# Gated cross-attention on one core: two squares placed five products later, and two steps of the last quad moved

## The chip, the cores and the metric

The kernel runs on one core of a Trainium2 chip. A core has a matrix engine (TensorE, in the profile PE, its weight loads PEld), a vector engine (VectorE, DVE), a scalar engine (ScalarE, ACT), a general engine (GpSimd, POOL) and a queue engine (SyncE, SP) that here only issues DMA transfers. Each engine works through its own list of instructions in order; semaphores make one wait for another. Matmul results go to PSUM, which is divided into banks; everything else lies in SBUF. The metric is the time of one execution on the device in microseconds (us); less is better.

## What is computed

Eight batches of 1024 tokens of width 1024 (x), and for each batch 64 memory rows of width 512:

```python
memory_proj = einsum('bme,de->bmd', memory, W_mem)
scores = einsum('bnd,bmd->bnm', hidden_states, memory_proj) / sqrt(D)
attn = softmax(scores, axis=-1)
memory_context = einsum('bnm,bmd->bnd', attn, memory_proj)
gate_input = concatenate([hidden_states, memory_context], axis=-1)
gate = sigmoid(einsum('bnf,df->bnd', gate_input, W_gate) + b_gate)
fused = hidden_states + gate * memory_context
out = fused * rsqrt(mean(fused ** 2, axis=-1) + 1e-6) * norm_w
```

All of it is in 32-bit floating point. Nearly all the arithmetic is the half of the gate's matmul that multiplies x with the first 1024 columns of W_gate.

## The kernel before

**Quads and products.** The 8192 tokens are worked on in 16 quads (`NQ`) of 512 tokens. In a quad, x times the gate's weights is done by a Strassen-like scheme: seven outer products, in the order `ORDER = (1, 6, 7, 5, 4, 2, 3)`, and inside each outer product seven inner products of 256 columns. An inner product is one slot of the schedule, so a quad has 49 slots (`SLOTS`), and outer products 1, 6, 7, 5, 4, 2 and 3 start at slots 0, 7, 14, 21, 28, 35 and 42 of the quad. A quad's four output tiles of 128 tokens are `O[q, 0]` to `O[q, 3]`, called gate in the profile; tiles 0 and 1 are row 0, tiles 2 and 3 row 1.

**One outer product** (`outer_product`, L880). Its first inner product fills a quarter of PSUM bank `af`, and ScalarE copies that to `u` (L901). The second goes to bank `kB`, the third to `kC`; VectorE adds each onto u in turn. Four more inner products accumulate in `ed` and again in `af`. The sixth and seventh reach the same `af` tile that the L901 copy reads, and so stand behind that copy. Steps on the output tiles follow: `pre` on GpSimd, `fin_ed` and `fin_af` on VectorE.

**The visits.** Row 1 is finished in product 4, row 0 in product 3 (`SECOND`). There, after the third inner product, TensorE makes a visit (`visit`, L820): a run of small matmuls with the attention, into banks `pc` and onto `af` and `ed`. They take the banks b and c that kB and kC used, so the VectorE adds onto u have to have read these. During the visit TensorE runs no inner product; this is the visit's gap. After it the sigmoid on ScalarE (L685), the product with pc on VectorE (`gated`), and what follows for the row.

**After a row is finished**, for all quads but the last: five slots later GpSimd issues a DMA that adds x from memory onto each tile (`residual`, L687). Later, ScalarE squares each of the two tiles with a sum along the row (`square`, L699) and takes the square root of both sums (L704, with its table load). VectorE takes the reciprocal (L710) and multiplies each half of a tile with it and with norm_w (`norm`, L714: halves (c, 0), (c, 1), (d, 0), (d, 1) of tiles c and d of the row); after the second half of a tile SyncE stores it to out. Row 0's steps fall in the next quad.

**The order of the work** is written by hand. `at(slot, ...)` puts a step on a list for a slot, and `step()` issues the list just ahead of that slot's matmuls; `mid(key, ...)` puts one at a fixed place inside an outer product: `(q, 4, 0)` is after the visit's matmuls have been issued and before `fin_af`, `(q, 3)` lies after the visit. The tuple `when` in `outer_product` holds the slots of the two squares and the four norms, counted from the end of product 3 or 4; `None` and -2 are places in the middle of the next quad's products 4 and 3, and -1 is `(q + 1, 4, 0)`. In a quad, the ones that matter here on ScalarE are the u copy of product 7 (slot 14), row 0's squares of the quad before (17, 18), the four attnT copies of the transposed attention (`transpose_attn`, slot 18, L472), and the u copies of products 5 and 4 (slots 21 and 28).

**The last quad** adds x by VectorE from a tile `xl`, which one DMA of 2 MB loads (`load_last`, L730; it takes the buffer of the quads' `xq`). Its norms follow slots of their own.

Of the kernel before, what the change touches and what calls it, by code (L numbers as in the profile page):

```python
# [20 lines left out]
def tile_gated_cross_attention_rmsnorm(  # L21
# [47 lines left out]
    NQ = B * QPB  # L69
# [546 lines left out]
    def at(slot, fn, *args):  # L616
        due.setdefault(slot, []).append(lambda: fn(*args))

    def mid(key, fn, *args):
        beside.setdefault(key, []).append(lambda: fn(*args))  # L620
# [5 lines left out]
    def plan(q):  # L626
        t0 = SLOTS * q
        nxt = q + 1 < NQ
        for i, o in enumerate(ORDER):
            for part, t in ((0, 1), (1, 2)):  # L630
                if i + 1 < len(ORDER):
                    at(t0 + 7 * i + t, inner_s, q, ORDER[i + 1], part)
                elif nxt:
                    at(t0 + 7 * i + t, inner_s, q + 1, ORDER[0], part)
        if q == 0:
            at(t0 + 7, scores, q)
            at(t0 + 8, add_scores, q)
        at(t0 + (3 if q else 7), outer_s, q, 3)
        at(t0 + (11 if q else 22), outer_s, q, 4)
        at(t0 + 9, transpose_scores, q)  # L640
        at(t0 + 10, softmax_a, q)
        at(t0 + 13, softmax_b, q)
        at(t0 + 18, transpose_attn, q)
        at(t0 + 22, attn_difference, q)
        if not nxt:
            at(t0 + 5, load_last)
            return
        at(t0 + 2, load_xq, q + 1)
        for i, t, half in (
            (20, 0, 0), (21, 1, 0), (23, 2, 0), (25, 3, 0), (37, 2, 1), (38, 3, 1), (42, 0, 1)  # L650
        ):
            at(t0 + i, transpose_x, q + 1, t, half)
        mid((q, 3, 1), transpose_x, q + 1, 1, 1)
        mid((q, 3), scores, q + 1)
        at(t0 + 46, add_scores, q + 1)
        mid((q, 3), outer_s, q + 1, 1)
        mid((q, 3), outer_s, q + 1, 2)
        if (q + 1) % QPB == 0:
            at(t0 + 10, load_mp, (q + 1) // QPB)
            at(t0 + 49, load_mg, (q + 1) // QPB)  # L660
        if q == 0:
            at(t0 + 8, add_bias, mgs[0][M:P, :])
            at(t0 + 20, add_bias, mgd[1, M:, :])
# [128 lines left out]
    def sqrt_table():  # L792

        t = t4k(small, [P, 1], "warm", "warm")
        pin(nc.scalar.activation(t, eps_sb, AF.Sqrt))
# [84 lines left out]
    def outer_product(q, o):  # L880
# [78 lines left out]
        if second and not nxt:  # L959
            c, d = 2 * row, 2 * row + 1  # L960
            if o == 3:
                sqrt_table()
            when = (3, 4, 4, None, 10, 11) if o == 4 else (0, 2, 2, 2, 3, 3)
            if o == 4:
                for h_ in range(2):
                    mid((q, 3, 0), last_weigh, c, h_)
            at(slot + when[0], last_root, d)
            at(slot + when[1], last_root, c)
            for w_, (t, h_) in zip(when[2:], ((d, 0), (d, 1), (c, 0), (c, 1))):
                if w_ is None:  # L970
                    mid((q, 3, 0), last_norm, t, h_)
                else:
                    at(slot + w_, last_norm, t, h_)
        elif second:

            c, d = 2 * row, 2 * row + 1
            for t in (d, c):
                at(slot + 5, residual, q, t)
            if row == 0:
                when = (17, 18, -1, None, 33, -2) if q + 2 < NQ else (17, 18, 20, 22, 24, 25)  # L980
            else:
                when = (17, 18, 22, 24, 29, 31)
            at(slot + when[0], square, q, c)
            at(slot + when[1], square, q, d)
            for w_, (t, h_) in zip(when[2:], ((c, 0), (c, 1), (d, 0), (d, 1))):
                if w_ is None:
                    mid((q + 1, 4), norm, q, t, h_)
                elif w_ < 0:
                    mid((q + 1, 4, 0) if w_ == -1 else (q + 1, 3), norm, q, t, h_)
                else:  # L990
                    at(slot + w_, norm, q, t, h_)
        del L2[q, o]

    for q in range(NQ):
        plan(q)
        for o in ORDER:
            outer_product(q, o)
# [29 lines left out]
```

## Time and profile before

| | |
|---|---|
| median of three executions | 956.16 us (955.21 to 956.31) |
| the profiled execution | 956.04 us |
| its span, first to last instruction | 954.0 us |
| TensorE's granted clock | 0.996 of full speed |
| ScalarE: squares, L699 | 60 of 1057 ns, idle before them 16.9 us |
| ScalarE: u copies, L901 | 112 of 364 ns |
| VectorE: norms, L714 | 120 of 987 ns |
| residual DMA, 512 KB | 60, median 8.4 us from issue to landing |
| xl DMA, 2 MB | one, 10.1 us from issue to landing |

The profile is of one execution; its span is 2.04 us shorter than the time of that execution. A group of instructions is named by the line of the kernel and by the tiles that it writes and reads, so that `gate<-in_x` is a residual, `junk<-gate` a square and `u<-af` a copy of the first inner product. A wait is put down to what came last by the profile. The ends of matmuls are modelled, so a busy TensorE isn't one at its peak; the distance between the starts of the same step in two quads is the better measure.

### The profile page before, as it was taken

How to read it: one execution, taken by the hardware profiler on the slowest of the kernel's cores; microseconds unless marked ns; L12 is line 12 of the kernel's file. 1: busy time of each engine (PE TensorE's matmuls, PEld its weight loads, DVE VectorE, ACT ScalarE, POOL GpSimd, SP SyncE). 2: the span in 40 equal slices, each digit the busy share in tenths (PEclk: the TensorE clock that was granted, in tenths of full speed). 3: DMA queues.
4: the chain of work that ended last, by engine and by line, in shares of the span. 5: the costliest groups of instructions: out<-in, count | busy, mean ns of one | idle time of the engine just before them, and what ended most of it. 6: DMA issues, size and time to landing. Idle time of an engine off the chain costs nothing.

```text
span 954.0 us, 15598 instructions
## 1 busy us (share of the span) xinstructions
PE 940.2 (99%) x5624; PEld 730.9 (77%) x5624; DVE 807.5 (85%) x1258; ACT 362.9 (38%) x782; POOL 710.3 (74%) x780
## 2 busy tenths in 40 slices
PE   9999999999999999999999999999999999999995
PEld 8546778787877778787877778687877778787773
DVE  6988888888888888888888888888888888888887
ACT  3001235262533425162433526252443526253456
POOL 4998877678676767788676767777686767877683
PEclk9999999999999999999999999999999999999998
DMA  9856674482919365481919365391918466390812
GB/s 377 276 151 156 110 127 107 114 174 54 200 45 193 96 135 120 109 179 44 212 45 178 89 144 133 91 196 30 217 53 164 103 131 146 77 211 25 220 66 89
DMA packets 70924, 128.41 MB, mean 135 GB/s; under 512 B 12352, under 2 KB 49216, under 8 KB 70592
## 3 DMA queue, kind: packets, MB, share of 16 engines
q1 hardware_dynamic: 61664, 93.86, 37.2%
q0 software_dynamic: 9184, 33.56, 19.2%
q8 instruction: 45, 0.74, 0.3%
q14 instruction: 31, 0.25, 0.1%
HBM read 87.56 MB, written 41.68 MB: 135 GB/s over the span
## 4 chain that ended last, share of the span: by engine, by line
PE 91%; DMA 4%; ACT 1%; DVE 1%; POOL 1%; issue 1%; SPq 0%; DVEq 0%
PE af L92 29%; PE ed L92 19%; PE pc L92 10%; PE kC L92 9%; PE kB L92 9%; PE pg L92 5%; PE psT_af L92 5%; DMA gate<-in_x 3%; PE pm L92 2%; POOL l L95 1%; DMA wm<-in_w_mem_t 1%; PE psT_ed L92 0%; ACT attnT L472 0%; PE psT_b L92 0%; DVE gate L714 0%
## 5 line engine op out<-in xcount | busy, mean ns | idle before, releaser
L95 POOL TENSOR_TENSOR gate<-gate,u 128x512 f32<-128x512 f32 (+1 forms) x224 | 237.0, 1071 | 189.7 <-DVE u L95 153.8
L685 ACT ACTIVATE gate<-gate 128x512 f32<-128x512 f32 x128 | 80.2, 630 | 224.3 <-DVE gate L95 224.3
L352 DVE STREAM_TRANSPOSE a<-xq 128x512 f32<-128x512 f32 x128 | 141.5, 1108 | 3.0 <-POOL it L95 3.0
L95 POOL TENSOR_TENSOR l<-a 128x256 f32<-128x256 f32 x128 | 112.9, 882 | 18.7 <-PE af L92 17.4
L714 DVE SCALAR_TENSOR_TENSOR gate<-gate,ss,nw_sb 128x512 f32<-128x512 f32 x120 | 118.4, 987 | 1.1
L92 PE MATMUL pc<-mg,attnT 64*64 64x512 f32 x512 | 116.8, 595 | 0.3 <-DVE u L95 0.3
L92 PE MATMUL ed<-it,l 128*128 128x256 f32 x448 | 115.0, 379 | 0.0
L92 PE MATMUL kB<-it,l 128*128 128x256 f32 x448 | 115.0, 379 | 0.0
L95 DVE TENSOR_TENSOR gate<-gate,pc 128x512 f32<-128x512 f32 x128 | 86.2, 682 | 31.7 <-ACT gate L685 31.7
L901 ACT COPY u<-af 128x256 f32<-128x256 f32 x112 | 40.8, 364 | 187.0 <-PE af L92 185.9
L92 PE MATMUL af<-w,a 128*128 128x256 f32 x384 | 98.5, 379 | 0.0
L92 PEld LDWEIGHTS kB<-it,l 128*128 128x128 f32 x448 | 85.1, 190 | 11.6
L95 DVE TENSOR_TENSOR gate<-gate,ed 128x512 f32<-128x512 f32 x112 | 76.1, 679 | 19.5 <-POOL gate L95 17.8
L92 PEld LDWEIGHTS ed<-it,l 128*128 128x128 f32 x448 | 83.9, 190 | 10.7
L95 DVE TENSOR_TENSOR gate<-gate,af 128x512 f32<-128x512 f32 (+1 forms) x128 | 76.9, 611 | 13.4 <-PE af L92 11.9
L92 PEld LDWEIGHTS af<-w,a 128*128 128x128 f32 x384 | 73.0, 190 | 10.3 <-issue 0.5
L95 POOL TENSOR_TENSOR l<-s 128x256 f32<-128x256 f32 x96 | 78.4, 816 | 3.1 <-PE af L92 3.1
L92 PEld LDWEIGHTS pc<-mg,attnT 64*64 64x64 f32 x512 | 32.9, 132 | 50.2 <-issue 23.5
L699 ACT ACTIVATE junk<-gate 128x1024 f32<-128x1024 f32 x60 | 63.5, 1058 | 16.9 <-DMA gate<-in_x 15.9
L92 PE MATMUL af<-mg,attnT 64*64 64x256 f32 (+1 forms) x384 | 67.4, 456 | 0.0
L92 PE MATMUL ed<-it,a 128*128 128x256 f32 x256 | 67.4, 386 | 0.0
L95 DVE TENSOR_TENSOR u<-u,kC 128x256 f32<-128x256 f32 x112 | 46.0, 410 | 23.7 <-PE kC L92 20.3
(147 smaller groups left out, 2043.4 us busy)
## 6 DMA issues: line engine op xcount, KB each, us to landing
xq<-in_x SPq DMA_DIRECT2D x64, 512.0 KB, 10.3
gate<-in_x POOLq DMA_DIRECT2D x60, 512.0 KB, 8.4
out<-gate SPq DMA_DIRECT2D x60, 512.0 KB, 3.0
w<-in_w_gate_t SPq DMA_DIRECT2D x8, 512.0 KB, 10.2
w<-in_w_gate_t SPq DMA_DIRECT2D x2, 2048.0 KB, 16.5
mg<-mgd SPq DMA_DIRECT2D x16, 256.0 KB, 5.5
wm<-in_w_mem_t SPq DMA_DIRECT2D x4, 512.0 KB, 6.0
mpd<-mpT SPq DMA_DIRECT2D x4, 512.0 KB, 7.7
```

The source lines that it names most:

```text
L92: pin(nc.tensor.matmul(o, lhsT, rhs, start=start, stop=stop, skip_group_check=True))
L95: pin(eng.tensor_tensor(o, a, b, op))
L352: nc.vector.transpose(A[key][:, :, r * P : (r + 1) * P], chunks(xq[q][:, 4 * t : 4 * t + 4, :], KD)[:, half * KH : (half + 1) * KH],)
L685: pin(nc.scalar.activation(g, g, AF.Sigmoid))
L699: nc.scalar.activation(junk, O[q, t], AF.Square, accum_out=ss[:, t % 2 : t % 2 + 1])
L714: nc.vector.scalar_tensor_tensor(g[:, cols], g[:, cols], rstd[:, t % 2 : t % 2 + 1], nw_sb[:, cols], ALU.mult, ALU.mult,)
L901: pin(nc.scalar.copy(p1, af[:, 0]))
```

## The change

```diff
@@ plan @@
         if not nxt:
-            at(t0 + 5, load_last)
+            at(t0 + 12, load_last)
             return
@@ outer_product @@
             if row == 0:
-                when = (17, 18, -1, None, 33, -2) if q + 2 < NQ else (17, 18, 20, 22, 24, 25)
+                when = (22, 23, -1, None, 33, -2) if q + 2 < NQ else (17, 18, 20, 22, 24, -1)
             else:
                 when = (17, 18, 22, 24, 29, 31)
```

Three things are moved, and none is added or taken away.

The squares of row 0 go from slots 17 and 18 of the next quad to slots 22 and 23. This holds for the rows of quads 0 to 13, which are squared in quads 1 to 14. On ScalarE the two squares, the load of the sqrt table and the sqrt stood between the u copy of product 7 and the attnT copies; now they stand behind the u copy of product 5 and ahead of that of product 4. The norms that use them keep their places.

In the last quad, `load_last` goes from slot 5 to slot 12. On SyncE the load of xl now stands behind the store of tile 2 of quad 14, and ahead of that of tile 3.

For row 0 of quad 14, which is finished in the last quad, the squares stay at 17 and 18; the fourth norm, the second half of tile 1, goes from slot 25 into the gap of product 4's visit. On VectorE it stood directly behind the third norm, ahead of the adds onto u of product 5's ed and of product 4's kB and kC; now it stands behind these and ahead of the first `fin_af`.

## The prediction

> **What bounds the kernel now.** I read the page first, then the windows by quad, the waits, the chain of waits, and last the timeline of single engines around each place. The page says that TensorE is the bound and that nothing else is near it:
>
> ```profile
> span 954.0 us, 15598 instructions
> ...
> PE 940.2 (99%) x5624; PEld 730.9 (77%) x5624; DVE 807.5 (85%) x1258; ACT 362.9 (38%) x782; POOL 710.3 (74%) x780
> ```
>
> So only time in which TensorE is kept from its next matmul can be won, and busy shares don't show it, since the ends of matmuls are modelled. I measured it by period. One quad goes from its first weight load for kB of product 1 to that of the next quad (16 starts, from the timeline of PEld). Five of these stretches, from the windows (span of the stretch, then PE busy, PEld, DVE, ACT, POOL, clock, DMA share, GB/s):
>
> ```profile
> 245.35:299.14 53.79, 53.79 (x337) 42.77 (x336) 45.99 (x75) 21.90 (x47) 39.90 (x47) 1.00 0.55 125
> 299.14:353.68 54.54, 54.03 (x337) 42.69 (x336) 45.54 (x75) 21.91 (x47) 39.93 (x47) 1.00 0.57 126
> 515.06:569.78 54.72, 54.03 (x338) 42.68 (x337) 45.57 (x75) 21.90 (x47) 39.95 (x47) 1.00 0.57 126
> 623.57:677.93 54.36, 54.02 (x337) 42.68 (x336) 45.55 (x75) 21.90 (x47) 39.89 (x47) 1.00 0.57 124
> 839.31:893.20 53.89, 53.89 (x338) 42.68 (x336) 45.76 (x75) 21.91 (x47) 39.92 (x47) 1.00 0.57 135
> ```
>
> The first row is the undisturbed period, 53.79 us; ten of the fourteen quads 1 to 14 have it within 0.01. Quads 4, 8, 10 and 14 are longer by 0.75, 0.93, 0.57 and 0.10, together 2.35 us. All four excesses lie between the kB of product 5 and that of product 4 (the other starts inside a quad repeat within 0.01). The waits name the chain there (waiter, what it waited for: total us, times, longest):
>
> ```profile
> ACT junk L699 <- DMA gate<-in_x: 15.9, 8, 2.8
> ...
> PE af L92 <- ACT u L901: 1.5, 3, 0.7
> ```
>
> ScalarE waits eight times for a residual DMA before a square, and three times TensorE then waits for ScalarE's copy of u. The timeline of quad 4 shows why (start, us):
>
> ```profile
> 313.03 0.35 ACT L901 COPY u<-af 128x256 f32<-128x256 f32 x1
> ...
> 316.05 1.06 ACT L699 ACTIVATE junk<-gate 128x1024 f32<-128x1024 f32 x1 [2.67 <-DMA gate<-in_x]
> ...
> 318.40 1.28 ACT L704 ACT_TABLE_LOAD   x1
> ...
> 320.00 1.51 ACT L472 COPY attnT<-pa 64x256 f32<-64x256 f32 x4
> ...
> 321.54 0.37 ACT L901 COPY u<-af 128x256 f32<-128x256 f32 x1
> ...
> 322.06 1.10 PE L92 MATMUL af<-t,l 128*128 128x256 f32 x4 [0.51 <-ACT u L901]
> ```
>
> The reader is to see a queue: the squares stand ahead of the attnT copies and of product 5's u copy, so a DMA that lands 2.67 us late (14.4 us in flight, by the chain of waits) pushes the u copy to 321.54, and TensorE may not accumulate on into that af bank until the copy has read it. The eight waits and the four excesses fit one rule: waits of 2.67, 2.85, 2.50 and 2.02 us cost 0.75, 0.93, 0.57 and 0.10, i.e. the wait less 1.92, and the other four (0.92 to 1.75) cost nothing. So 1.92 us is the slack of this queue, and the excess has no second source.
>
> **What the Trainium skill says.** "DMA: Bandwidth & Descriptors", section "Issuing engines are not separate DMA queues": transfers issued by SyncE and by GpSimd run on the same 16 engines and interleave. The trace agrees: the transfers of gate tiles, 512 KB for a residual, land after 2.0 to 14.6 us (median of the residuals 8.4), and the 14.4 us one falls in a quad where mg and four xq loads were issued just before (293.93 to 296.98); so its time is not the kernel's to fix. "ScalarE: Activation LUTs", section "What ACT_TABLE_LOAD costs": about 1283 ns for a table load, 186 ns + 0.833 ns an element for an ACTIVATE with immediate scale and bias, so an estimated 1.04 us for a square of 1024; the trace has 1.28 and 1.06. "SBUF — State Buffer", section "Who interferes with whom": a VectorE instruction with two SBUF inputs contends with a GpSimd one that reads SBUF. The norm reads gate and nw_sb, and its spread here, 744 to 1759 ns, fits that.
>
> **Part 1: the squares five products later (quads 1 to 14).** Moved on ScalarE: two squares, their accumulator reads, a sqrt table load, a sqrt; POOL, PE and SP keep their order there. In quad 3, without a wait, that block runs 259.70 to 263.64, so 3.94 us. It now stands behind the u copy of product 5. That copy can start about 1.06 after its first matmul (product 6: matmul 304.54, copy 305.60); product 5's starts at 263.27, so copy 264.33 to 264.70, i.e. 19.35 after the quad's start. Does the DMA still hold it? The three late residuals landed at 316.05, 532.14 and 640.30, while the block is now reached at 299.14, 515.06 and 623.57 plus 19.35, i.e. 318.49, 534.41 and 642.92: spare 2.4, 2.3 and 2.6 us. So the wait goes, and the u copy is ahead of it anyway. What is late next: the u copy of product 4 at 270.44 and, on VectorE, the reciprocal of the norm at 272.45. The block ends at 264.70 + 3.94 = 268.64, 1.8 and 3.8 us before them. The cover is thus 1.8 us, plus about 0.5 until VectorE's kB add (271.32 against the copy's end at 270.81). Gain: 2.35 us. Bounds: 1.2 if half of the stalls come back by later landings, 2.4 if even the 0.01s go.
>
> **Part 2: xl at slot 12 instead of 5.** On SP one DMA of 2 MB changes places with one out store: before at 887.45, landing 10.1 us later; now behind the store at 902.75, so it lands near 913, against a first use at 924.77. Nothing waits on SP behind it but stores whose tiles nobody needs again. The residuals issued at 895.06 lose a 2.5 us overlap with xl and gain perhaps as much at the other end; their squares at 907.34 did not wait. Cost 0, bounds ±0.1.
>
> **Part 3: the fourth norm of quad 14 in the visit's gap.** Before, VectorE's backlog in quad 15 is the chain (905 to 922: norms, attnT differences, u sums), and the visit of product 4 starts late:
>
> ```profile
> 917.07 2.42 DVE L714 SCALAR_TENSOR_TENSOR gate<-gate,ss,nw_sb 128x512 f32<-128x512 f32 x2
> ...
> 919.75 0.41 DVE L95 TENSOR_TENSOR u<-u,kB 128x256 f32<-128x256 f32 x1
> ...
> 920.21 0.65 PE L92 MATMUL pc<-mg,attnT 64*64 64x512 f32 x2 [0.29 <-DVE u L95]
> ...
> 921.44 0.69 DVE L95 TENSOR_TENSOR gate<-gate,af 128x512 f32<-128x512 f32 x1 [0.76 <-PE af L92]
> ```
>
> Quad 15's interval from product 4's kB to product 2's is 0.36 longer than elsewhere. One norm (1.2 us) less ahead of the kB add frees it: the add then follows its matmul by 1.13 as in quad 4 (918.03 + 1.13 = 919.16, not 919.75), and the visit starts 0.36 earlier, at 919.85. The norm isn't gone, though: it now stands between the kC add and fin_af. In quad 3, with a norm in the same gap, fin_af comes 1.80 after the visit's first pc matmul instead of 1.23; 0.19 of that is a reciprocal which is not moved here. So fin_af at 919.85 + 1.61 = 921.46, as before (921.44). From there to the visit of product 3 VectorE runs without an idle microsecond that TensorE could shorten (its waits are for ScalarE's sigmoids, themselves behind it), and that visit waits for the kB add ending at 935.93. It started at 936.10; the earlier one started 0.05 after its add, so there is 0.12 of slack. TensorE keeps 0.12 of the 0.36 and gives 0.24 back there. With the norm at 0.75 (nothing on POOL) it keeps 0.36; at 1.76, the longest, VectorE is late by 0.55 and 0.43 is lost. I take 0.1, since POOL was busy through that gap before (918.91 to 921.99).
>
> **Sum.** 2.35 + 0 + 0.1 = 2.45 us. The profiled execution took 956.04 us (span 954.0, 2.04 around it): 951.55 + 2.04 = 953.6. It stands 0.12 below the median shown, 956.16, which gives 953.7. I forecast 953.7 us.
>
> **Rivals.** *Half comes back.* Landings differ from execution to execution (three runs spread over 1.1 us), and the medians may hold fewer stalls than this profile, or residuals may land later once the squares no longer pace the quads. For it: eight of fourteen waited. Against it: 2.3 us spare at the worst landing seen. Gain 1.2: 955.0. *The last quad takes it back.* The norm runs 1.76 us against POOL, VectorE's chain to the second visit is 0.55 late: gain 2.35 - 0.43 = 1.9, 954.2; for it the 1.79 us norm at 933.48, against it 1.2 us in both quads where I looked at that gap. *Slower: ScalarE's block overruns.* Five products later the block has 5.74 us (264.70 to 270.44) instead of running into slack; if its start or its length slips by more than 1.8 + 0.5 us, product 4's u copy, kB add and visit are late in every one of fourteen quads. At 0.5 each that costs 7 us against the 2.45: 960.7. It decides from a landing some 4.6 us later than the worst seen (2.3 + 2.3), or a block of 6.2 us instead of 3.94; nothing in the trace reaches half of that. *More:* all of part 3 and jitter, 953.2.
>
> **How the numbers follow.** A measurement of this kernel can tell about 0.2% from no change, 1.9 us: faster is below 954.25, slower above 958.07. Forecast 0.68 (953.3 to 954.2, all faster); more 0.07 (faster); last quad takes it back 0.06 (about half on each side of the line); half comes back 0.15 (within); slower 0.04. Faster 0.68 + 0.07 + 0.03 = 0.78, same 0.03 + 0.15 = 0.18, slower 0.04. The range must leave out no more than 0.2: from 953.0, under the jitter of the best case, to 954.9, just short of the middle of "half comes back".
>
> **What would show it.** Right: quads 4, 8, 10, 14 at 53.79; no wait of ScalarE's squares of tiles 0 and 1 for the DMA in quads 1 to 14, and the first square 19.35 us after the quad's start; product 4's u copy still waiting for TensorE; in quad 15 the first visit 0.36 earlier, the second waiting for VectorE. Wrong: any quad over 53.9, a square's wait that is still there, a u copy of product 4 directly behind the sqrt, or quad 15's first fin_af more than 1.8 us after its visit's first pc matmul.

## The result, and the profile after

The changed kernel takes 953.78 us (median of 14 executions, 953.38 to 954.53) beside 955.97 us for the kernel before (14 executions, 955.02 to 958.29): a ratio of 0.9978, with a 95% interval of 0.9971 to 0.9986. The forecast was 953.7. The profiled execution took 953.63 us, 1.85 of it outside the span. The page of the changed kernel, its first lines and the shares of the chain that ended last:

```profile
span 951.8 us, 15584 instructions
...
PE 939.9 (99%) x5624; PEld 732.1 (77%) x5624; DVE 806.5 (85%) x1258; ACT 361.9 (38%) x782; POOL 711.0 (75%) x780
...
PE 97%; DVE 2%; ACT 1%; issue 0%; DVEq 0%
```

The busy times hardly differ from those before. The chain does: DMA had 4% of it and TensorE 91%; now DMA has none. The windows of the changed kernel, from the first kB weight load of one quad to that of the next, for quads 3, 4, 8, 10 and 14 (columns as in the prediction):

```profile
245.67:299.46 53.79, 53.79 (x338) 42.76 (x336) 45.88 (x75) 21.79 (x47) 39.90 (x47) 1.00 0.56 125
299.46:353.25 53.79, 53.79 (x338) 42.77 (x336) 45.90 (x75) 21.79 (x47) 39.90 (x47) 1.00 0.56 124
514.63:568.42 53.79, 53.79 (x338) 42.77 (x337) 45.97 (x75) 21.80 (x47) 39.93 (x47) 1.00 0.58 126
622.21:676.00 53.79, 53.79 (x338) 42.76 (x336) 45.95 (x75) 21.79 (x47) 39.91 (x47) 1.00 0.58 126
837.38:891.17 53.79, 53.79 (x338) 42.76 (x337) 45.98 (x75) 21.79 (x47) 39.94 (x47) 1.00 0.50 113
```

The four long quads are gone; all of quads 1 to 14 have 53.79 or 53.80. ScalarE's wait for a residual (15.9 us, 8 times) and TensorE's for the u copy (1.5 us, 3 times) no longer occur among the waits. The timeline of ScalarE in quad 3 shows the block in its new place (start, us):

```profile
261.20 1.51 ACT L472 COPY attnT<-pa 64x256 f32<-64x256 f32 x4 [1.30 <-PE pa L461]
264.71 0.37 ACT L901 COPY u<-af 128x256 f32<-128x256 f32 x1 [2.00 <-PE af L92]
264.98 1.06 ACT L699 ACTIVATE junk<-gate 128x1024 f32<-128x1024 f32 x1
...
268.62 0.30 ACT L704 ACTIVATE ss<-ss,eps_sb 128x2 f32<-128x2 f32 x1
270.75 0.37 ACT L901 COPY u<-af 128x256 f32<-128x256 f32 x1 [1.83 <-PE af L92]
```

The u copies of products 5 and 4, ahead of the block and behind it, both wait for TensorE and not the other way round.

The residuals themselves did not land earlier. In quad 4 of the changed kernel, the issue of the two on GpSimd and the summary of their landings:

```profile
301.32 1.76 POOL L689 DMA_DIRECT2D gate<-in_x  x2
...
DMA to landing us min/median/max: 12.1/13.4/14.8
```

The second one, issued at 301.96, lands at 316.8, 17.34 us after the quad's start; the one of quad 4 before had landed 16.88 after it. ScalarE now reaches the squares 19.31 us after the quad's start, behind that landing. By the old rule, a landing later than 16.15 us after the quad's start costs its excess (16.90 less 0.75, from quad 4 before). Six of the fourteen landings of this execution are later than that, the latest at 17.37; in the old order they would have cost 5.0 us, by this estimate. So it is the place of the wait that changed, not the wait's cause.

The span is the sum of three stretches. From the first kB of quad 0 to that of quad 15: 813.03 us before, 810.69 after, so 2.34 won. From there to the end: 60.75 and 60.61, 0.14 won. Ahead of it: 80.17 and 80.48, 0.31 lost. The last is probably not the change: over the 13 profiled executions of this study, whose setup has the same steps, it took anything from 80.17 to 81.46 us, with GpSimd's wait for the first load of `wm` (5.5 to 6.9 us) among what differs. Together the span is 2.17 shorter (953.95 to 951.78); the execution is 2.41 shorter, since it has 0.24 less outside the span.

### The profile page after: what moved, and what is told of

It reads as the page before. It is cut to its first block, busy times and chain, and to the rows that moved or that the text cites. A ratio compares the mean times of both kernels' runs of the same rounds, so it can differ in the third digit from the quotient of the medians.

```text
span 951.8 us, 15584 instructions
## 1 busy us (share of the span) xinstructions
PE 939.9 (99%) x5624; PEld 732.1 (77%) x5624; DVE 806.5 (85%) x1258; ACT 361.9 (38%) x782; POOL 711.0 (75%) x780
## 4 chain that ended last, share of the span: by engine, by line
PE 97%; DVE 2%; ACT 1%; issue 0%; DVEq 0%
PE af L92 31%; PE ed L92 21%; PE pc L92 10%; PE kC L92 10%; PE kB L92 10%; PE pg L92 5%; PE psT_af L92 5%; PE pm L92 3%; DVE gate L95 1%; PE psT_ed L92 0%; PE pz L92 0%; DVE gate L788 0%; PE sc L430 0%; PE pa L461 0%; PE psT_b L92 0%; PE pt L193 0%
## 5 line engine op out<-in xcount | busy, mean ns | idle before, releaser
L95 POOL TENSOR_TENSOR l<-a 128x256 f32<-128x256 f32 x128 | 110.9, 866 | 18.6 <-PE af L92 17.5
L92 PE MATMUL af<-t,s 128*128 128x256 f32 x256 | 65.8, 379 | 0.0
```

What stands on the lines that cost most here:

```text
L92: pin(nc.tensor.matmul(o, lhsT, rhs, start=start, stop=stop, skip_group_check=True))
L95: pin(eng.tensor_tensor(o, a, b, op))
```

## The experiments

Each kernel is compared by its time and by these stretches, since the setup alone moves the time by up to 1.3 us. "Quad 15" is its distance from product 4's kB to product 2's (10.20 us before, 9.84 after), with the starts of its two visits after the kB of product 4 (2.40 and 2.03) and of product 3 (2.04 and 2.25).

**One part alone: the squares.** On the kernel before:

```diff
-                when = (17, 18, -1, None, 33, -2) if q + 2 < NQ else (17, 18, 20, 22, 24, 25)
+                when = (22, 23, -1, None, 33, -2) if q + 2 < NQ else (17, 18, 20, 22, 24, 25)
```

> The squares alone are moved (slots 22 and 23), the last quad is as before. Theory: all but 0.15 us of the gain is here; quads 1 to 14 have 53.79 us each, quad 15 keeps its 0.36 us ahead of product 2's kB, the median is 2.3 us below the kernel before. Rival (the last quad brings a good part of it): the gain is 1.5 us or less.

Measured: 953.88 us (14 executions), ratio 0.9979 (0.9971 to 0.9987). From quad 0 to quad 15 it has the 810.69 us of the full change; quad 15 keeps its 10.22. So the squares give all of the gain that the time can show.

**The other two parts without the squares.** On the changed kernel, `(22, 23, ...)` back to `(17, 18, ...)`:

> The two moves of the last quad alone, squares at 17 and 18 as before. Theory: stalls in some of quads 4, 8, 10 and 14 remain, each the wait of the first square for its DMA less 1.92 us; in quad 15 the visit of product 4 is 0.36 earlier and that of product 3 late by 0.2, so the median is 0.1 to 0.2 us below the kernel before, not to be told from none. Rival: 0.5 us or more.

Measured: 955.74 us (13 executions), ratio 0.9994 (0.9986 to 1.0002), not told apart from no change. Quad 15 has 9.84, with visits at 2.03 and 2.25. In this execution eleven squares waited for a residual, 18.4 us in all. The windows of the four long quads (6, 8, 10 and 14):

```profile
406.92:461.03 54.11, 54.03 (x337) 42.68 (x336) 45.55 (x75) 21.90 (x47) 39.90 (x47) 1.00 0.58 127
514.82:569.30 54.48, 54.03 (x337) 42.68 (x336) 45.56 (x75) 21.89 (x47) 39.94 (x47) 1.00 0.57 126
623.10:677.45 54.35, 54.03 (x338) 42.68 (x337) 45.76 (x75) 21.90 (x47) 39.97 (x47) 1.00 0.58 125
838.82:893.58 54.76, 54.03 (x337) 42.69 (x336) 45.55 (x75) 21.90 (x47) 39.94 (x47) 1.00 0.50 110
```

They are 0.32, 0.69, 0.56 and 0.97 over 53.79, behind waits of 2.25, 2.62, 2.49 and 2.90: each wait less 1.93. The seven waits up to 1.87 cost nothing. The prediction's rule (wait less 1.92) thus holds for another draw of landings. The draw itself differs: quads 6, 8, 10, 14 here, 4, 8, 10, 14 in the kernel before; the stalls add up to 2.54 us here.

**The norm alone.** On the kernel before, only the last 25 becomes -1 (the load of xl stays at slot 5):

> The kernel before with the fourth norm alone moved into the visit's gap. Theory: in quad 15 the visit of product 4 is 0.36 us earlier, the visit of product 3 waits 0.2 us more for VectorE's kB add; 0.15 us in all. If xl has a part in it, these differ from the changed kernel's.

Measured in one execution: 956.29 us. Quad 15 has 9.84, 2.03 and 2.26, as with the load moved too. So the later load of xl has no part in quad 15. This execution is also a third draw for the rule: waits of 2.96, 2.53 and 1.95 us cost 1.04, 0.60 and 0.03, and six up to 1.69 cost nothing.

**How far must the squares go?** Two slots later, on the kernel before: `(19, 20, -1, None, 33, -2)`, behind the attnT copies but still ahead of product 5's u copy.

> The squares at slots 19 and 20, so behind the attnT copies but still ahead of product 5's u copy; the last quad as before. Theory (the u copy of product 5 has a deadline, 1.92 us after its end in an undisturbed quad of the kernel before): the block starts 3.0 us later, at or after the landings seen, and the u copy then ends 1.5 us later than in the kernel before without a wait, 0.4 us ahead of the deadline, so no quad is longer than 53.79 and the gain is the same 2.3 us, with 0.4 us of cover left. Rival (the block has to be behind that u copy): the stalls stay, 14 quads are longer, no gain or a loss.

Measured: 953.86 us (14 executions), ratio 0.9980 (0.9972 to 0.9988), the same as five products later; no wait for a residual, quads 1 to 14 at 53.79. The rival fell. The block starts 16.94 us after the quad's start, where it had started at 14.14 in an undisturbed quad, and that was only just enough: in quad 10 the landing came at 17.01 and the square at 17.03. It has less to spare: product 5's u copy starts 20.91 after the quad's start, 1.87 later than in the changed kernel. In quad 4 of the kernel before it was 3.36 later and cost 0.75, so 2.61 are free and 0.74 of them are left (0.4 expected). The latest landing of the changed kernel, 17.37, would have used 0.4 of these.

**Too far.** On the changed kernel, `(29, 30, -1, None, 33, -2)`: behind product 4's u copy.

> The change with the squares seven slots later still (29 and 30), behind product 4's u copy; everything else as changed. Theory: the block now ends 274.8 us into the frame of quad 3, 2.3 us after the norm in the visit's gap wants its square root, and the sigmoid's table load comes after it; VectorE and the sigmoids are 2.3 to 4 us late in each of quads 1 to 14, and TensorE waits 0.5 to 2 us in each for the banks of product 5 or for pc: 7 to 28 us slower than the changed kernel. Rival (a block anywhere behind product 5's u copy does): same as the changed kernel.

Measured: 968.72 us (4 executions), ratio 1.0134 (1.0120 to 1.0148), 14.9 above the changed kernel. Each of quads 1 to 14 takes 54.85, so 1.06 more. The waits of this kernel (waiter, what it waited for: total us, times, longest):

```profile
DVE ss L710 <- ACT ss L704: 30.7, 14, 2.4
...
PEld af L92 <- POOL l L95: 14.1, 14, 1.1
...
PE af L92 <- ACT u L901: 8.9, 14, 0.7
```

The size lies in the range expected and the first step is as expected: VectorE's reciprocal waits 2.2 a quad for the square root. But TensorE isn't held where I expected it. Product 4's visit is on time; most of the loss lies in product 2, whose kB comes 6.91 before product 3's instead of 6.04, and another 0.2 in product 3. ScalarE and TensorE in quad 3 of this kernel:

```profile
284.45 0.63 ACT L685 ACTIVATE gate<-gate 128x512 f32<-128x512 f32 x1 [3.35 <-DVE gate L95]
286.43 0.63 ACT L685 ACTIVATE gate<-gate 128x512 f32<-128x512 f32 x1 [1.35 <-DVE gate L95]
286.97 0.35 ACT L901 COPY u<-af 128x256 f32<-128x256 f32 x1
...
287.46 1.10 PE L92 MATMUL af<-w,l 128*128 128x256 f32 x4 [0.64 <-ACT u L901]
```

What was queued behind the reciprocal on VectorE comes late, and so do the sigmoids that wait for it. Product 2's u copy stands behind the last of these sigmoids on ScalarE; it starts 3.97 us after that product's kB, in the changed kernel 2.04. TensorE may go on in af only after it, and starts 0.14 after the copy's end. The profile puts the load of these matmuls' weights down to GpSimd's sums l; these belong to product 3 by the order of the work, and the last one that had ended, at 287.24, ended ahead of the copy. So again a u copy is late in ScalarE's queue, one product further on.

**Dose of the landing.** Row 0's residual is issued four slots later, once on the kernel before and once on the changed kernel; both have this edit:

```diff
-                at(slot + 5, residual, q, t)
+                at(slot + (9 if row == 0 and q + 2 < NQ else 5), residual, q, t)
```

> The kernel before with the residuals of row 0 issued at slot 9 instead of 5, between two of GpSimd's sums for product 7, about 4.4 us later; nothing else is moved (the last quad keeps slot 5). Theory: each first square waits until its DMA lands; a wait of w costs w less 1.92 us. If the transfers take as long as before, the waits grow by 4.4 us and quads 1 to 14 are longer by 1 to 5 us each, 20 to 45 us in all; since they meet less of the xq loads they may land sooner, so at least 5 us slower. Rival (the stalls are not from this wait): within 1 us of the kernel before.

Measured: 964.62 us (4 executions), ratio 1.0089 (1.0072 to 1.0105), 8.5 above the kernel before. That fits "at least 5 us slower", but by luck: the waits for a residual became fewer and not longer, three with a sum of 3.7 us in the profiled execution, and the time was lost elsewhere, as the second run shows.

> The changed kernel with the same later residuals (slot 9). Theory: the worst landing of the kernel before was 2.3 us ahead of the block's new place; 4.4 us later it is 2.1 us behind it, and the block then ends 0.3 us after product 4's u copy wants to start, which VectorE's 0.5 us covers: no quad longer than 53.9 us, the time within 0.5 us of the changed kernel. The block's cover is 1.8 us against the DMA at its new place, so a wait above 2.3 us would cost its excess. Rival (the change only moved the stall): 5 us slower or more, as without the change.

Measured: 962.79 us (4 executions), ratio 1.0075 (1.0061 to 1.0088). This misses my expectation, within 0.5 us of the changed kernel, by 8.5 us. From product 5's kB to product 4's, where the waits cost before, it takes 6.04 us in every quad, and no square waits. The loss is one product earlier: product 7's kB to product 5's takes 6.89 instead of 6.26, in both kernels and in each of quads 1 to 14, and 14 times 0.62 is 8.7 us. The timeline of quad 4, kernel with the late issue on the changed one:

```profile
307.26 1.78 POOL L689 DMA_DIRECT2D gate<-in_x  x2
308.43 1.38 POOL L95 TENSOR_TENSOR l<-a 128x256 f32<-128x256 f32 x1
309.28 1.20 POOL L95 TENSOR_TENSOR l<-a,l 128x256 f32<-128x256 f32 x1
...
309.75 2.50 DVE L714 SCALAR_TENSOR_TENSOR gate<-gate,ss,nw_sb 128x512 f32<-128x512 f32 x1
312.18 0.41 DVE L439 TENSOR_REDUCE mx<-sc 128x4 f32<-128x256 f32 x1
```

and the same place of VectorE in the changed kernel:

```profile
308.20 0.75 DVE L714 SCALAR_TENSOR_TENSOR gate<-gate,ss,nw_sb 128x512 f32<-128x512 f32 x1
308.87 0.42 DVE L439 TENSOR_REDUCE mx<-sc 128x4 f32<-128x256 f32 x1
```

The issue of the two DMAs now stands between GpSimd's sums of product 7 and holds back the last two of them, which start 1.17 and 2.02 us after that product's kB instead of 0.01 and 0.70 (kB at 307.26 here, at 305.72 in the changed kernel). The last one thus still runs when VectorE's norm starts, and the norm takes 2.50 us instead of 0.75. The softmax's maximum behind it comes 4.92 us after product 7's kB instead of 3.15, and the softmax is 1.8 us late. Its end meets the transposes of the attention, where TensorE now waits, two times a quad:

```profile
PEld pa L461 <- ACT e L454: 10.8, 28, 0.4
```

So neither kernel measures a late landing alone. Nor was there much of a dose. Relative to the quad's start, the second residual was issued 4.3 us later (6.83 us after it instead of 2.50) and landed, in the mean of quads 1 to 14, 0.6 us later on the kernel before (15.56 instead of 14.99) and 0.3 us earlier on the changed kernel (15.49 instead of 15.75). Its time in flight fell from a median of 12.9 and 13.4 us to 8.9 and 8.8.

The three waits of the late kernel on the one before, 1.71, 0.89 and 1.08 us, cost 0.91, 0.10 and 0.29: each the wait less 0.8, not less 1.92. The softmax, which stands ahead of the block on ScalarE, is 1.8 us late there while product 5 is only 0.62 late, so 1.92 less 1.2 is left of the slack, about 0.7 by this estimate. The form of the rule holds; its slack belongs to the schedule. The changed order has no wait there, but its latest landing, 16.80 us after the quad's start, was no later than those before. That the new order absorbs a landing later than the latest drawn, by as much as the 2.3 us claimed, is therefore not tested by a landing. The next three runs test the other side of its slack, the length of the block.

**Dose of the block.** Ahead of the sqrt in `square`, extra squares of the same tile into `junk`, which nothing reads; two and four on the changed kernel, three on the kernel before:

```diff
+        if t == 1 and q + 2 < NQ:
+            for _ in range(2):
+                pin(nc.scalar.activation(junk, O[q, t], AF.Square))
```

> The changed kernel with two more squares of tile 1 (results unused) in ScalarE's block of each of quads 1 to 14, behind the two real ones: the block is 1.93 us longer (two of 1057 ns that overlap by 0.09). Theory: the block has 1.83 us of cover ahead of product 4's u copy, and that copy 0.5 us ahead of VectorE's kB add; the copy is 0.1 us late and no quad is longer than 53.79 us, the time within 0.3 us of the changed kernel. Rival (ScalarE's block is already on the path): 1.9 us a quad, 27 us slower.

Measured with two: 954.52 us (12 executions), ratio 0.9988 (0.9979 to 0.9996). The median is 0.74 above the changed kernel's, more than the 0.3 expected. No quad is longer: from the first kB on, the span is 871.31 us against 871.30. In the profiled execution the whole difference of the span is the setup, 81.46; the other executions have no profile, and the fastest of them, 953.70, is 0.32 above the fastest of the changed kernel. The u copy behind the block starts 0.25 us late (0.1 expected), and nothing waits for it.

> The same with four more squares, 3.86 us. Theory: the block overruns its cover, product 4's u copy is 2.0 us late and the kB add 1.5 us, and the visit of product 4 comes 1.2 to 1.5 us late in each of 14 quads: 17 to 21 us slower than the changed kernel. This is the price of the slower rival of the prediction. Rival (there is more cover behind the u copy): under 5 us.

Measured with four: 977.89 us (4 executions), ratio 1.0232 (1.0215 to 1.0250); the span is 975.7 us. Each quad is 1.72 longer, 24.1 us in fourteen. Timeline of quad 3:

```profile
270.49 4.33 ACT L705 ACTIVATE junk<-gate 128x1024 f32<-128x1024 f32 x4
...
276.33 0.35 ACT L904 COPY u<-af 128x256 f32<-128x256 f32 x1
...
276.72 0.42 DVE L95 TENSOR_TENSOR u<-u,kB 128x256 f32<-128x256 f32 x1 [2.55 <-ACT u L904]
```

The four took 4.33 us where I had reckoned with 3.86, so the loss is above the range expected; where it falls is as expected, VectorE's kB add waits for the copy, and product 4's visit for the add. The copy is 2.44 us late, the add 1.94 and the visit 1.73, so 4.33 less 1.72 leaves 2.6 us of cover. The mechanism of the prediction's slower rival is thus real: in the changed kernel it lacks only its trigger.

> The kernel before with three more squares of tile 1 in the block of each of quads 1 to 14, 2.9 us. Theory (1.92 us of slack in the queue ahead of product 5's u copy, whatever fills it): a quad without a DMA wait is longer by 2.9 - 1.92 = 0.98 us, one with a wait of w by 0.98 + w; with waits that sum to 14 to 18 us, 28 to 32 us slower than without any stall, so 982 to 986 us. Rival (only late DMAs do harm, for instance through contention): within 2 us of the kernel before.

Measured with three on the kernel before: 996.26 us (4 executions, 992.37 to 1001.52), ratio 1.0427 (1.0388 to 1.0466), 10 us more than expected. The part on ScalarE fits: quads without a wait take 55.03, so 1.24 over, and three squares of 3.24 us less the 1.92 of slack are 1.32. Quads with a wait should lose the wait on top; six of them lost 1.6 to 3.1 us more than that, 14.0 us in all in this execution. One with a wait of 1.75 lost 4.78 in place of 2.99. Windows of that stretch, cut where the trace's record of the granted clock changes:

```profile
216.00:219.53 3.53, 0.68 (x4) 0.28 (x3) 0.95 (x3) 3.29 (x7) 0.00 (x0) 1.00 0.00 0
219.53:220.76 1.23, 1.23 (x6) 1.10 (x7) 1.23 (x2) 0.00 (x0) 0.00 (x0) 1.00 0.00 0
220.76:224.17 3.41, 3.41 (x10) 2.70 (x9) 1.72 (x4) 0.28 (x1) 2.94 (x3) 0.50 0.00 0
224.17:226.00 1.83, 1.83 (x12) 1.28 (x14) 0.61 (x2) 1.38 (x2) 1.75 (x4) 1.00 0.00 0
```

The column after POOL is the granted clock: 1.2 us after the end of the stall it falls to 0.50, for 3.4 us. Half of these, 1.7 us, is about what the quad lost beyond the rule, 1.8. The six quads that lost more are the six with such a drop. The stall and the slow matmuls are in the timeline of the same kernel:

```profile
219.53 1.10 PE L92 MATMUL af<-t,l 128*128 128x256 f32 x4 [2.85 <-ACT u L904]
220.47 1.62 PE L92 MATMUL af<-t,s 128*128 128x256 f32 x4
221.89 1.92 PE L92 MATMUL af<-t,a 128*128 128x256 f32 x4
```

So the old place of the squares is as sensitive to ScalarE's length as the rule says, and more so where the stall is long. The rival, that only late DMAs do harm, fell: the quads without a wait are longer, too.

**The fourth norm later still.** On the changed kernel, slot 48 in place of the visit's gap: `(17, 18, 20, 22, 24, 48)`.

> The changed kernel with the fourth norm of quad 14 put ahead of the last inner product (slot 48 of quad 15) instead of the visit's gap. Theory: VectorE's chain between the two visits of quad 15 starts 0.25 us earlier, so the second visit no longer waits and TensorE keeps all 0.36 us, 0.2 more than the changed kernel; the norm takes the 0.73 us in which VectorE waits for the last matmul, and overruns it by 0 to 0.5. Together 0.2 us faster to 0.3 us slower than the changed kernel, which shows where that norm is cheapest. Rival (VectorE is not what holds the second visit): the second visit stays 0.2 us late.

Measured: 954.78 us (21 executions), ratio 0.9986 (0.9979 to 0.9992), 1.0 above the changed kernel where at most 0.3 was expected; quads 1 to 14 are the same. `fin_af` comes 1.23 after the visit's first pc matmul, 0.26 earlier than in the changed kernel, as expected. But the second visit starts 2.67 after its kB, not earlier but 0.42 later. Timeline of this kernel in quad 15:

```profile
923.06 1.27 POOL L95 TENSOR_TENSOR gate<-gate,u 128x512 f32<-128x512 f32 x1
...
923.09 1.79 DVE L95 TENSOR_TENSOR gate<-gate,xl 128x512 f32<-128x512 f32 x1
```

and of the changed kernel:

```profile
922.40 0.99 DVE L95 TENSOR_TENSOR gate<-gate,xl 128x512 f32<-128x512 f32 x1
...
922.79 1.73 POOL L95 TENSOR_TENSOR gate<-gate,u 128x512 f32<-128x512 f32 x1
```

and of the kernel before, which has no norm in that gap either:

```profile
924.77 0.69 DVE L95 TENSOR_TENSOR gate<-gate,xl 128x512 f32<-128x512 f32 x1
...
924.83 1.76 POOL L95 TENSOR_TENSOR gate<-gate,u 128x512 f32<-128x512 f32 x1
```

VectorE's addition of xl now starts 0.03 us behind GpSimd's step on gate and takes 1.79 us. In the kernel before it had started 0.06 us ahead and took 0.69; in the changed kernel it starts 0.39 ahead and takes 0.99. It was not VectorE that moved: after `fin_af` VectorE waits for TensorE's ed, and of the 0.26 won only 0.03 is left where the addition starts (4.56 after the visit's first pc matmul, 4.58 in the changed kernel). GpSimd came 0.45 earlier (4.53 against 4.98), without the norm beside its steps. So most of the gain expected was lost at ed, and the order of two starts made a loss of it. A further 0.75 us lies at the very end: the span ends 4.21 us after VectorE's last norm, 3.47 in the changed kernel. One store more is among the last ones, seven instead of six, but what held the end isn't shown, nor that all executions have it: the fastest, 953.80, is 0.42 above the fastest of the changed kernel.

## Why the prediction was right, point by point

**What bounds it.** The stalls of quads 4, 8, 10 and 14 were foreseen to be worth 2.35 us and all to go; 2.34 went (813.03 to 810.69). That they come from ScalarE's queue, and not from something that happened beside it, is shown twice: with the squares alone moved they are gone, and with all but the squares moved they stay and obey the same rule with a slack of 1.93. That the stalls of one profile are the typical ones was taken without a test, and came out well: three executions in the old order had 2.34, 2.54 and 1.66 us of them.

**Part 1.** The first square was expected 19.35 us after the quad's start; it is at 264.98 - 245.67 = 19.31. The cover to the u copy behind the block was put at 1.8 us, and that copy still waits 1.83 for TensorE. The cover beyond it was put at about 0.5. With four extra squares it shows itself: the copy is 2.44 us late and the add 1.94, so 0.5 lie between them as put; another 0.2, which was not counted, lie between the add and the visit. The residuals' spare time was put at 2.3 us, from the landings of one execution. In the changed kernel the latest landing, 17.37 us after the quad's start, is 1.94 ahead of the first square at 19.31: enough, but less than claimed, and no run delayed a landing until it was used up. The time in flight was called not the kernel's to fix. The place of the issue does set it (median 12.9 or 13.4 us from slot 5, 8.9 or 8.8 from slot 9), only the landing hardly moves. This is in line with the Trainium skill, "DMA: Bandwidth & Descriptors", section "Issuing engines are not separate DMA queues": transfers of all issuers interleave on the same engines. That the xq loads issued ahead are what holds the residuals is not shown by a run. Five slots were not needed: two give the same time, with 0.74 us to spare for the copy. The prediction did not ask what the smallest sufficient move is.

**Part 2.** xl was expected to be issued at 902.75 and to land near 913. It was issued at 901.2 and landed 9.3 us later, at 910.5, ahead of a first use at 922.4. Cost 0, as taken.

**Part 3.** The 0.36 us at the first visit came out exactly (10.20 to 9.84). Then `fin_af` was expected 1.61 after the visit's first pc matmul, and comes 1.48 after it. The timeline of VectorE and TensorE in the changed kernel's quad 15:

```profile
917.92 0.42 DVE L95 TENSOR_TENSOR u<-u,kC 128x256 f32<-128x256 f32 x1 [0.37 <-PE kC L92]
918.26 1.11 DVE L714 SCALAR_TENSOR_TENSOR gate<-gate,ss,nw_sb 128x512 f32<-128x512 f32 x1
919.30 0.67 DVE L95 TENSOR_TENSOR gate<-gate,af 128x512 f32<-128x512 f32 x1
...
917.82 0.65 PE L92 MATMUL pc<-mg,attnT 64*64 64x512 f32 x2
...
933.45 0.41 DVE L95 TENSOR_TENSOR u<-u,kB 128x256 f32<-128x256 f32 x1
...
933.91 0.65 PE L92 MATMUL pc<-mg,attnT 64*64 64x512 f32 x2
```

The norm took 1.11 us there where the 1.23 of quad 3 was assumed. At the second visit the add ends at 933.86 and the visit starts 0.05 later: the 0.12 of slack is used up and VectorE now is the bound there, as foreseen. Of the 0.36, 0.21 is given back (0.24 expected) and 0.15 kept (0.12). Had the gap been judged by the length of the norm alone, as my expectation for slot 48 did, the sign would have been wrong: whether VectorE's addition starts ahead of GpSimd's step decides. The Trainium skill says so in "SBUF — State Buffer", section "Who interferes with whom": "Issue order, not op shape, decides who blocks." The runs agree: one addition took 0.69 us when it started 0.06 us ahead of GpSimd's step and 1.79 when it started 0.03 behind it.

**The sum.** 2.34 + 0.14 stands beside the 2.45 forecast. That the profiled execution became 2.41 shorter is partly chance, as the setup gave 0.31 away and the part outside the span 0.24 back. The medians, 955.97 and 953.78, are 2.19 apart. That the median meets the forecast to 0.1 us has luck in it: the median of three that it started from was 0.19 above the median of fourteen, which offsets most of the 0.26 that the gain fell short.

**The rivals.** "Half comes back" is excluded by the quads: none of the fourteen keeps a stall, here and in the other profiled executions with the squares at this place and no extra squares beside them. Later landings, one reason given for it, did come (17.37 against 17.06 at the latest), and cost nothing. "The last quad takes it back" needed a norm of 1.76 and met one of 1.11. "ScalarE's block overruns" has the mechanism, as four extra squares show, but a block 2.17 us longer still costs nothing in any quad.

## What to carry to other kernels

In an engine that works in order, a step that waits for a DMA should not stand ahead of a copy that has a deadline, at a place where its wait can outlast the copy's slack. Moving it behind the copy cost nothing here, since two things had slack: the next copy (1.8 us, and 2.6 until TensorE stands still) and the step's own readers. Both can be estimated from the timeline before the move; where the first was overrun (four extra squares) or the second (squares behind product 4's copy), each quad lost 1.7 and 1.1 us. Measure such stalls as the distance between the same step in successive periods, and check the rule (wait less slack) on each period: the busy shares hardly differ here, and the medians show that 2.2 us are gone but not where. Before shifting a step of GpSimd or VectorE, look at which of the two starts first where both read SBUF, and not at the sum of their work.

## What the runs showed of the hardware that was not expected

- With three extra squares on the kernel before, TensorE had a stall for product 5's u copy in each of quads 1 to 14. All six stalls of 2.85 to 3.98 us were followed by a granted clock of 0.50, for 3.4 us (2.85, 3.02 and 3.04) or 6.8 us (3.07, 3.39 and 3.98); a stall of 2.79 us and seven of 1.00 to 1.35 were not. The Trainium skill, "TensorE: Matmul & The Clock Gate", section "What's actually happening", puts this state behind at least one idle window of about 3.4 us; by this one execution, whose stalls are reckoned from modelled ends of matmuls, less is enough.
- Two DMA issues on GpSimd held its next sums back by 1.16 and 1.32 us. Between two pairs of sums they cost TensorE 0.62 us a quad, by way of a VectorE norm that became 1.75 us longer.
- Issuing the residuals 4.3 us later moved their mean landing by 0.6 us later on one kernel and 0.3 us earlier on the other: some 4 us of their time in flight went away.
- A shift of 0.09 us between VectorE's addition of xl and GpSimd's step, from 0.06 ahead to 0.03 behind, made the addition 1.10 us longer.
- Squares of one tile into one tile, back to back on ScalarE, took 1.08 us each (4.33 for four); I had counted on a small overlap.
